# A graph network's two attention layers: the sums over edge slots move from VectorE reductions to identity products of TensorE in PSUM

## The chip, the cores and the metric

The kernel runs on one core of a Trainium2 chip. The metric is the device time of one execution in microseconds (us). The kernel before has a median of 5291.32 us over 3 runs, which lie between 5290.82 and 5300.97 us. The engines that matter here are TensorE (PE in the profile; its weight loads have a row of their own, PEld), VectorE (DVE), ScalarE (ACT) and GpSimd (POOL), which issues the gathers.

## The reference

Four message-passing layers run one after the other over the same graph of 3125 nodes and 100000 edges, each followed by a residual sum and a layernorm. Layers 0 and 1 are not touched. Layer 2 is attention with four heads and an edge bias, layer 3 attention with one head and keys that depend on the edge's type. Cut to what matters:

```python
# layer 2 (H = 4 heads of 32)
attn = jnp.sum(Q[dst] * K[src], axis=-1) * SCALE + edge_attr @ We      # then leaky
attn_exp = jnp.exp(attn - jnp.max(attn))
attn_norm = attn_exp / jnp.maximum(jax.ops.segment_sum(attn_exp, dst, n)[dst], 1e-12)
agg = jax.ops.segment_sum(V[src] * attn_norm[:, :, None], dst, n)
# layer 3 (one head; k_t is the key after the matrix of the edge's type)
scores = jnp.sum(Q[dst] * k_t, axis=-1) / scale * mu[edge_type]
out = jax.ops.segment_sum(V[src] * softmax_over_dst(scores)[:, None], dst, N)
```

For every destination node the kernel has to sum the value rows of its incoming edges, each weighted by its softmax weight. That weighted sum is what the change rearranges.

## The kernel before

The nodes are sorted by degree and cut into 25 tiles of 128, one node to a partition. A node's edges become slots: tile t has `CAP[t]` slots (57 in the first tile, 21 in the last, 821 in all), and slot s of a tile holds the s-th edge of each of its 128 nodes. Slots are worked through in chunks of at most W = 8. Nodes with more edges than slots would be finished in a loop (`behind`), which makes no trip on these inputs: the profile has 821 gathers a layer.

For each slot GpSimd issues one indirect gather (L102) that brings a row of 256 floats, key and value, for each of the 128 nodes into the tile `kv`. Layer 2 has 8 `kv` buffers, layer 3 has 12, each of one chunk; a buffer comes free when its value half has been read. On VectorE a chunk then takes these steps: `qk`, keys times query (L1206 in layer 2, L1364 in layer 3); `lg`, the sum over the head's columns (L1207, L1365); then, once per run, the softmax bookkeeping (`weights`, L700 to L714, with the exponentials on ScalarE); and, per chunk again, `weigh` (L722 to L730), in which `msg` is value times weight (L725), `u` is the sum of `msg` over its slots (L729), and `u` is added to the tile's sum `accb` (L730). Before a run's messages `faded` (L720) multiplies `accb` by the correction for a grown maximum. The query `qp` and the weights `ex` lie in PSUM, `kv`, `msg`, `u` and `accb` in SBUF. `msg` has two buffers, `u` one.

A run is a softmax group: in layer 2 `segments` makes runs of at most three chunks, in layer 3 a run is a whole tile. In layer 2 each tile ends with `closing` (L1252 to L1266: transposes, two dense layers, layernorm) and `table3` (L1274 to L1290: the queries of layer 3 and the key and value rows for all eight edge types, by products of TensorE), and a scatter of these rows into `ktv_tab`, which GpSimd issues. In layer 3 each tile ends with a division, a layernorm, and a scatter into `out`, also by GpSimd; in the source it stands after the gathers of the next tile.

Nobody writes the order of instructions on an engine by hand: a scheduler interleaves them by its own costs, and each engine then runs its list strictly in order. So a gather that waits for a free `kv` buffer, or a scatter that waits for its rows, holds back every gather behind it, and a VectorE instruction that waits holds back all of VectorE's.

[...]

Of the kernel before, what the change touches and what calls it, by code (L numbers as in the profile page):

```python
# [8 lines left out]
F32 = mybir.dt.float32  # L9
# [9 lines left out]
P = 128  # L19
# [8 lines left out]
W = 8  # L28
# [59 lines left out]
def tile_gnn(ctx, tc, a, out):  # L88
# [629 lines left out]
    def faded(acc, corr, heads):  # L718
        acch = acc.rearrange("p (h d) -> p h d", h=heads)
        V.tensor_mul(acch, acch, corr.unsqueeze(2).to_broadcast([P, heads, D // heads]))  # L720

    def weigh(pool, acc, val, ex, n, heads):  # L722

        msg = pool.tile([P, W, D], F32, name="msg")
        V.tensor_tensor(msg[:, :n, :].rearrange("p s (h d) -> p s h d", h=heads),  # L725
                        val.rearrange("p s (h d) -> p s h d", h=heads),
                        ex.unsqueeze(3).to_broadcast([P, n, heads, D // heads]), op=OP.mult)
        u = pool.tile([P, D], F32, name="u", bufs=1)
        V.tensor_reduce(u, msg[:, :n, :].rearrange("p s d -> p d s"), AX.X, OP.add)  # L729
        V.tensor_add(acc, acc, u)  # L730

    def query(ps, q):

# [454 lines left out]
    with tc.tile_pool(name="l2", bufs=2) as wp, tc.tile_pool(name="l2s", bufs=1) as sp, \  # L1188
# [31 lines left out]
        def behind2(t, pl, mk, rl):  # L1220
            lg = wp.tile([P, max(CAP), H2], F32, name="lg")
            kv = rows2(query(ps1, qb[:, t, :]), pl, W, lg[:, :W])
            biased(pl, W, lg[:, :W], mk)
            ex = ps1.tile([P, max(CAP), H2], F32, name="ex")
            corr = softmax(wp, lg[:, :W], W, H2, m[:, t, :], l[:, t, :], ex[:, :W])
            faded(accb[:, t, :], corr, H2)
            weigh(wp, accb[:, t, :], kv[:, :, D:], ex[:, :W], W, H2)

        behind(wp, behind2)

# [38 lines left out]
        def table3(t):  # L1269


            of = wp.tile([P, NTY, P], F32, name="of", bufs=1)
            for k in range(NTY):
                V.tensor_scalar(of[:, k, :], ident, is_t[:, k, t:t + 1], None, op0=OP.mult)  # L1274
            xk_ps = ps1.tile([P, NTY, P], F32, name="xk_ps", tag="dense")
            T.matmul(xk_ps, xb[:, t, :], of, start=True, stop=True)  # L1276
            xkT = wp.tile([P, NTY, P], F32, name="xkT", bufs=1)
            A.activation(xkT, xk_ps, AF.Copy)
            p_ps = ps1.tile([P, 3 * D], F32, name="p_ps")
            for k in range(NTY):  # L1280
# [12 lines left out]

        for t in range(NT):
            qp = query(ps1, qb[:, t, :])
            for s0, s1, run in segments(t):
                lg = wp.tile([P, max(CAP), H2], F32, name="lg")
                parts = []
                for c0, w in run:
                    o = OFF[t] + c0  # L1300
                    parts.append(rows2(qp, pay_sb[:, o:o + w], w, lg[:, c0 - s0:c0 - s0 + w]))
                n, o = s1 - s0, OFF[t] + s0
                biased(pay_sb[:, o:o + n], n, lg[:, :n], mask[:, o:o + n])
                ex = ps1.tile([P, max(CAP), H2], F32, name="ex")
                corr, rest = weights(wp, lg[:, :n], n, H2, m[:, t, :], l[:, t, :], ex[:, :n])
                faded(accb[:, t, :], corr, H2)
                for (c0, w), kv in zip(run, parts):
                    weigh(wp, accb[:, t, :], kv[:, :w, D:], ex[:, c0 - s0:c0 - s0 + w], w, H2)
                rest()

            rl = wp.tile([P, H2], F32, name="rl")
            V.tensor_scalar(rl, l[:, t, :], 1e-12, None, op0=OP.max)
            V.reciprocal(rl, rl)
            closing(t, rl)
            table3(t)
# [34 lines left out]
    with tc.tile_pool(name="l3", bufs=2) as wp, tc.tile_pool(name="l3s", bufs=1) as sp, \  # L1350
# [17 lines left out]
        def behind3(t, pl, mk, rl):  # L1368
            lg = wp.tile([P, max(CAP), 1], F32, name="lg")
            kv = rows3(query(ps1, qb[:, t, :]), pl, W, lg[:, :W, 0])  # L1370
            V.tensor_add(lg[:, :W, 0], lg[:, :W, 0], mk)
            ex = ps1.tile([P, max(CAP), 1], F32, name="ex", bufs=2)
            corr = softmax(wp, lg[:, :W], W, 1, m[:, t, :], l[:, t, :], ex[:, :W])
            faded(accb[:, t, :], corr, 1)
            weigh(wp, accb[:, t, :], kv[:, :, D:], ex[:, :W], W, 1)

        behind(wp, behind3)

# [1 line left out]
        for t in range(NT):  # L1380
            n = CAP[t]
            qp = query(ps1, qb[:, t, :])
            lg = wp.tile([P, max(CAP), 1], F32, name="lg")
            parts = []
            for s0, w in chunks(t):
                o = OFF[t] + s0
                parts.append(rows3(qp, pay_sb[:, o:o + w], w, lg[:, s0:s0 + w, 0]))
            V.tensor_add(lg[:, :n, 0], lg[:, :n, 0], mask[:, OFF[t]:OFF[t + 1]])
            ex = ps1.tile([P, max(CAP), 1], F32, name="ex", bufs=2)
            if to_put is not None:  # L1390

                unordered("out", scatter(out, od.ids(to_put[0]), to_put[1], bounds_check=N - 1, oob_is_err=False),
                          "nodes differ")
            corr, rest = weights(wp, lg[:, :n], n, 1, m[:, t, :], l[:, t, :], ex[:, :n])
            faded(accb[:, t, :], corr, 1)
            for (s0, w), kv in zip(chunks(t), parts):
                weigh(wp, accb[:, t, :], kv[:, :w, D:], ex[:, s0:s0 + w], w, 1)
            rest()
            rl = wp.tile([P, 1], F32, name="rcl")
            V.tensor_scalar(rl, l[:, t, :], 1e-10, None, op0=OP.add)  # L1400
            V.reciprocal(rl, rl)  # L1401
            y = wp.tile([P, D], F32, name="y")
            V.scalar_tensor_tensor(y, accb[:, t, :], rl, xb[:, t, :], op0=OP.mult, op1=OP.add)  # L1403
            o = wp.tile([P, D], F32, name="o")
            layernorm(wp, o, y, t)
            to_put = t, o
# [20 lines left out]
```

## Time and profile before

| what | value |
|---|---|
| median of 3 runs | 5291.32 us |
| profiled execution | 5349.01 us |
| its span, first to last instruction | 5347.3 us |
| DVE busy over the span | 3023.3 us (57%) |
| POOL busy over the span | 2812.4 us (53%) |
| PE busy over the span | 2126.7 us (40%) |
| gathers of layer 2, first to last | from 2806.4 to 4013.9 us |
| gathers of layer 3, first to last | from 4112.5 to 5286.7 us |
| sums `u` (L729) in both layers | 228 reductions, 384.1 us |

The profiled execution is 58 us (1.1%) slower than the median, so a sum made on the profile is carried over to the median by a factor of 0.99. Layers 0 and 1 end shortly before 2806 us. From there on there are four stretches: layer 2's gathers, the end of layer 2 after its last gather, layer 3's gathers, and the end after the last gather. In the profile a row of a group gives the busy time, the mean time of one instruction in ns, and after the bar the idle time of the engine just before these instructions, with what ended most of it. "remote" and "issue" are releasers that the profile cannot name. In a timeline the columns are start, duration, engine, line, operation, tiles, count, and in brackets the idle time before.

### The profile page before, as it was taken

The page shows a single profiled execution, that of the slowest core. Times are in us where ns is not written, and L with a number is a line of the kernel's source. Part 1 is how long each engine was busy: PE and PEld are TensorE (multiplying, and loading weights), DVE is VectorE, ACT ScalarE, POOL GpSimd, SP SyncE. Part 2 cuts the span into 40 slices and gives each one's busy share as a digit, 9 for nine tenths or more (in the row PEclk, how much of TensorE's full clock was granted, in tenths as well). Part 3 has the DMA queues.
Part 4 walks back from the last instruction along what each step waited for, and adds up shares of the span by engine and source line. Part 5 has one row for each costly group of instructions (what it writes and reads, how often), then busy time and mean ns, then how long its engine had stood idle before and what let it go on. Part 6 is the DMA issues. An engine that isn't in the chain of part 4 may idle for free. (4 is left out here: it accounts for less than half of the span.)

```text
span 5347.3 us, 40354 instructions
## 1 busy us (share of the span) xinstructions
PE 2126.7 (40%) x11946; PEld 1387.3 (26%) x12091; DVE 3023.3 (57%) x7369; ACT 985.1 (18%) x2562; POOL 2812.4 (53%) x2897
## 2 busy tenths in 40 slices
PE   7256767765666676776660121222323000000000
PEld 5134545544444444454330010011111000000000
DVE  8346665664555566555424566666664454454656
ACT  1023332322232333232110011111111000000000
POOL 0545545555353443444017666666662777666664
PEclk9577887777777778777885555555556555555555
DMA  2423323333222222333333333333331333223332
GB/s 84 121 72 86 95 75 91 89 92 87 79 83 77 79 82 69 89 85 86 148 137 104 102 98 114 103 105 106 121 113 61 105 98 92 86 85 92 89 88 60
DMA packets 213055, 498.40 MB, mean 93 GB/s; under 512 B 62329, under 2 KB 109100, under 8 KB 208185
## 3 DMA queue, kind: packets, MB, share of 16 engines
q0 software_dynamic: 136448, 397.65, 25.9%
q1 hardware_dynamic: 76344, 97.76, 5.7%
q8 instruction: 102, 1.67, 0.1%
q14 instruction: 161, 1.32, 0.1%
HBM read 424.65 MB, written 70.63 MB: 93 GB/s over the span
## 5 line engine op out<-in xcount | busy, mean ns | idle before, releaser
L102 POOL DMA_INDIRECT hs<-h_tab,srcx x821 | 844.9, 1029 | 839.2 <-issue 392.4
L102 POOL DMA_INDIRECT kv<-kv_tab,pay_sb x821 | 782.2, 953 | 372.2 <-issue 245.2
L102 POOL DMA_INDIRECT kv<-ktv_tab,pay_sb x821 | 803.0, 978 | 320.0 <-issue 243.7
L729 DVE TENSOR_REDUCE u<-msg 128x128 f32<-128x1024 f32 (+4 forms) x228 | 384.1, 1685 | 161.2 <-remote 100.0
L880 PE MATMUL zps<-oh,zq 128*128 128x512 bf16 x1099 | 357.7, 438 | 41.4 <-DVE bn_sd L751 10.1
L831 PE MATMUL lg<-yw,low 128*128 128x8 f32 x1642 | 234.7, 269 | 175.9 <-issue 88.6
L102 POOL DMA_INDIRECT zs<-z_tab,rel x205 | 208.8, 1019 | 172.9 <-DVE az L851 56.7
L831 PEld LDWEIGHTS lg<-yw,low 128*128 128x128 f32 x1642 | 228.6, 212 | 224.5 <-issue 107.1
L893 DVE TENSOR_TENSOR hs<-hs,t_ps 128x408 f32<-128x408 f32 (+1 forms) x231 | 122.1, 529 | 283.3 <-remote 165.8
L892 PE MATMUL t_ps<-zw,zT 128*128 128x136 f32 x1232 | 224.3, 311 | 127.5 <-DVE hs L893 78.9
L622 ACT ACTIVATE c_oha<-c_oha,srclo 128x50 bf16<-128x50 bf16 (+2 forms) x821 | 205.8, 346 | 250.1 <-DVE c_oha L570 147.0
L725 DVE TENSOR_TENSOR msg<-kv,ex 128x1024 f32<-128x1024 f32 (+4 forms) x228 | 248.8, 1103 | 3.1 <-issue 2.5
L884 PE MATMUL pre<-zT,zw 128*128 128x512 f32 x308 | 203.6, 748 | 89.0 <-ACT zT L882 44.3
L892 PEld LDWEIGHTS t_ps<-zw,zT 128*128 128x128 f32 x1232 | 193.4, 212 | 159.3 <-DVE hs L893 109.2
L740 PE MATMUL tp<-ident,an 128*128 128x128 f32 x25 | 11.5, 459 | 525.2 <-DVE qk L1206 257.0
L648 PE MATMUL c_ps<-c_ohs,c_ohd 128*128 128x128 bf16 x1300 | 128.6, 247 | 211.2 <-ACT c_sb L650 92.2
L886 PEld LDWEIGHTS pre<-ident,hs 128*128 128x128 f32 x1232 | 189.1, 221 | 74.0 <-issue 71.6
L1276 PE MATMUL xk_ps<-of,xqb 128*128 128x512 f32 x50 | 51.9, 1141 | 386.3 <-DVE xqb L758 239.6
L829 ACT ACTIVATE low<-pre 128x512 f32<-128x512 f32 (+2 forms) x215 | 123.2, 574 | 421.8 <-PE pre L886 148.0
L822 PE MATMUL pre<-identb,hq 128*128 128x512 bf16 (+3 forms) x645 | 199.3, 408 | 2.1 <-ACT hq L814 0.8
L886 PE MATMUL pre<-ident,hs 128*128 128x128 f32 x1232 | 194.5, 305 | 0.4 <-issue 0.4
L1364 DVE TENSOR_TENSOR qk<-kv,qp 128x1024 f32<-128x1024 f32 (+4 forms) x114 | 126.5, 1110 | 114.9 <-DMA kv<-ktv_tab,pay_sb 98.4
(397 smaller groups left out, 5206.3 us busy)
## 6 DMA issues: line engine op xcount, KB each, us to landing
rb<-rel_tab SPq DMA_DIRECT2D x77, 256.0 KB
c_tab<-c_sb SPq DMA_DIRECT2D x25, 768.0 KB
cs<-c_tab SPq DMA_DIRECT2D x6, 3200.0 KB
hs<-h_tab,srcx POOLq DMA_INDIRECT x821
kv<-kv_tab,pay_sb POOLq DMA_INDIRECT x821
kv<-ktv_tab,pay_sb POOLq DMA_INDIRECT x821
h_tab<-h SPq DMA_DIRECT2D x25, 132.0 KB
zs<-z_tab,rel POOLq DMA_INDIRECT x205
```

Of the source, the lines that this page charges most:

```text
L102: return G.indirect_dma_start(out=dst, out_offset=None, in_=table, in_offset=indirect(idx), **kw)
L622: A.activation(oha[:, s // 2, 0, :, s % 2], oha[:, s // 2, 1, :, s % 2], AF.Copy, scale=srclo[:, o:o + 1])
L648: T.matmul(cps[:, j * P:(j + 1) * P], ohd[:, b // 2, :, b % 2], ohs[:, b // 2, :, b % 2], start=(i == 0), stop=(i == nb - 1))
L725: V.tensor_tensor(msg[:, :n, :].rearrange("p s (h d) -> p s h d", h=heads), val.rearrange("p s (h d) -> p s h d", h=heads), ex.unsqueeze(3 ...
L729: V.tensor_reduce(u, msg[:, :n, :].rearrange("p s d -> p d s"), AX.X, OP.add)
L822: T.matmul(pre[:, :k], hq[:, i, :], identb.unsqueeze(1).to_broadcast([P, k, P]), start=(i == 0), stop=False)
L831: T.matmul(lg_ps[:, s, :], low[:, s, :], yw8, start=True, stop=True)
L880: T.matmul(zps, zq[:, i, 2 * R * k2:2 * R * (k2 + 1)], ohs[i][:, cols], start=(i + k2 == 0), stop=(i == NK - 1 and k2 == 1))
L884: T.matmul(pre[:, :k], zw[:, :D], zT[:, cols], start=False, stop=False)
L886: T.matmul(pre[:, s, :], hs[:, s0 + s, :D], ident, start=False, stop=(s == k - 1))
L892: T.matmul(t_ps[:, s, :], zT[:, (s0 + s) * P:(s0 + s + 1) * P], zw[:, D:], start=True, stop=True)
L1364: V.tensor_mul(qk[:, :n], kv[:, :n, :D], qp.unsqueeze(1).to_broadcast([P, n, D]))
```

## The change

`weigh` no longer reduces and adds on VectorE. It makes `msg` as before, and then one TensorE product per slot, with the 128x128 identity as the weights and `msg` of that slot as the moving operand (both float32), adds the slot into a PSUM bank `u_ps`. The first product of a run starts the bank, the last one stops it. VectorE adds `u_ps` to `accb` once per run. In layer 3 the fading of `accb` and the addition become one instruction. To have a bank for `u_ps` in layer 2, `p_ps` moves into the two banks of `e_ps`. `u_ps` has one buffer in layer 2 and two in layer 3.

```diff
-    def weigh(pool, acc, val, ex, n, heads):
+    def weigh(pool, u_ps, val, ex, n, heads, first, last):
 
         msg = pool.tile([P, W, D], F32, name="msg")
         V.tensor_tensor(msg[:, :n, :].rearrange("p s (h d) -> p s h d", h=heads),
                         val.rearrange("p s (h d) -> p s h d", h=heads),
                         ex.unsqueeze(3).to_broadcast([P, n, heads, D // heads]), op=OP.mult)
-        u = pool.tile([P, D], F32, name="u", bufs=1)
-        V.tensor_reduce(u, msg[:, :n, :].rearrange("p s d -> p d s"), AX.X, OP.add)
-        V.tensor_add(acc, acc, u)
+        for s in range(n):
+            T.matmul(u_ps, ident, msg[:, s, :], start=(first and s == 0), stop=(last and s == n - 1))
...
-            p_ps = ps1.tile([P, 3 * D], F32, name="p_ps")
+            p_ps = ps1.tile([P, 3 * D], F32, name="p_ps", tag="e_ps", bufs=2)
...
                 faded(accb[:, t, :], corr, H2)
+                u_ps = ps1.tile([P, D], F32, name="u_ps")
                 for (c0, w), kv in zip(run, parts):
-                    weigh(wp, accb[:, t, :], kv[:, :w, D:], ex[:, c0 - s0:c0 - s0 + w], w, H2)
+                    weigh(wp, u_ps, kv[:, :w, D:], ex[:, c0 - s0:c0 - s0 + w], w, H2, c0 == s0, c0 + w == s1)
                 rest()
+                V.tensor_add(accb[:, t, :], accb[:, t, :], u_ps)
...
             corr, rest = weights(wp, lg[:, :n], n, 1, m[:, t, :], l[:, t, :], ex[:, :n])
-            faded(accb[:, t, :], corr, 1)
+            u_ps = ps1.tile([P, D], F32, name="u_ps", bufs=2)
             for (s0, w), kv in zip(chunks(t), parts):
-                weigh(wp, accb[:, t, :], kv[:, :w, D:], ex[:, s0:s0 + w], w, 1)
+                weigh(wp, u_ps, kv[:, :w, D:], ex[:, s0:s0 + w], w, 1, s0 == 0, s0 + w == n)
             rest()
+            V.scalar_tensor_tensor(accb[:, t, :], accb[:, t, :], corr, u_ps, op0=OP.mult, op1=OP.add)
```

The loops `behind2` and `behind3` are changed in the same way.

More of the change, by code (lines that the diff above doesn't have):

```diff
@@ L1226, in behind2 @@
             faded(accb[:, t, :], corr, H2)
-            weigh(wp, accb[:, t, :], kv[:, :, D:], ex[:, :W], W, H2)
+            u_ps = ps1.tile([P, D], F32, name="u_ps")
+            weigh(wp, u_ps, kv[:, :, D:], ex[:, :W], W, H2, True, True)
+            V.tensor_add(accb[:, t, :], accb[:, t, :], u_ps)
         behind(wp, behind2)
@@ L1306, in tile_gnn @@
                 faded(accb[:, t, :], corr, H2)
+                u_ps = ps1.tile([P, D], F32, name="u_ps")
                 for (c0, w), kv in zip(run, parts):
-                    weigh(wp, accb[:, t, :], kv[:, :w, D:], ex[:, c0 - s0:c0 - s0 + w], w, H2)
+                    weigh(wp, u_ps, kv[:, :w, D:], ex[:, c0 - s0:c0 - s0 + w], w, H2, c0 == s0, c0 + w == s1)
                 rest()
+                V.tensor_add(accb[:, t, :], accb[:, t, :], u_ps)
             rl = wp.tile([P, H2], F32, name="rl")
@@ L1374, in behind3 @@
             faded(accb[:, t, :], corr, 1)
-            weigh(wp, accb[:, t, :], kv[:, :, D:], ex[:, :W], W, 1)
+            u_ps = ps1.tile([P, D], F32, name="u_ps", bufs=2)
+            weigh(wp, u_ps, kv[:, :, D:], ex[:, :W], W, 1, True, True)
+            V.tensor_add(accb[:, t, :], accb[:, t, :], u_ps)
         behind(wp, behind3)
@@ L1394, in tile_gnn @@
             corr, rest = weights(wp, lg[:, :n], n, 1, m[:, t, :], l[:, t, :], ex[:, :n])
[L1395 removed]
+            u_ps = ps1.tile([P, D], F32, name="u_ps", bufs=2)
             for (s0, w), kv in zip(chunks(t), parts):
[L1397 removed]
+                weigh(wp, u_ps, kv[:, :w, D:], ex[:, s0:s0 + w], w, 1, s0 == 0, s0 + w == n)
             rest()
+            V.scalar_tensor_tensor(accb[:, t, :], accb[:, t, :], corr, u_ps, op0=OP.mult, op1=OP.add)
             rl = wp.tile([P, 1], F32, name="rcl")
```

## The prediction

> **What bounds the kernel now.** I read the page's slices first. Layers 2 and 3 are the right half: TensorE is nearly or wholly idle there, its clock is at half, and POOL and VectorE share the work.
>
> ```profile
> PE   7256767765666676776660121222323000000000
> DVE  8346665664555566555424566666664454454656
> POOL 0545545555353443444017666666662777666664
> PEclk9577887777777778777885555555556555555555
> ```
>
> Next the stretches of the two layers: layer 2's gathers, its end, layer 3's gathers, the end.
>
> ```profile
> 2806.00:4015.00 1209.00, 268.04 (x493) 119.31 (x493) 723.01 (x1544) 149.19 (x331) 803.04 (x842) 0.56 0.36 107
> 4015.00:4112.00 97.00, 43.82 (x85) 19.08 (x85) 57.08 (x141) 21.63 (x43) 3.89 (x4) 0.66 0.12 46
> 4112.00:5288.00 1176.00, 0.00 (x0) 0.00 (x0) 600.55 (x928) 47.25 (x112) 824.62 (x842) 0.50 0.32 93
> 5288.00:5347.00 59.00, 0.00 (x0) 0.00 (x0) 46.51 (x93) 5.23 (x11) 3.98 (x4) 0.50 0.02 6
> ```
>
> The columns are length, then busy time (count) of PE, PEld, DVE, ACT, POOL, then PEclk, DMA share, GB/s. Neither engine looks full, so I ask for POOL's and VectorE's groups in each stretch (layer 2 first in both fences).
>
> ```profile
> L102 POOL DMA_INDIRECT kv<-kv_tab,pay_sb x821 | 782.2, 953 | 372.2 <-issue 245.2 <-DVE bn_mv L749 33.1 <-DVE msg L725 28.6
> L102 POOL DMA_INDIRECT kv<-ktv_tab,pay_sb x821 | 803.0, 978 | 320.0 <-issue 243.7 <-remote 32.1 <-DVE msg L725 19.8
> ```
> ```profile
> L729 DVE TENSOR_REDUCE u<-msg 128x128 f32<-128x1024 f32 (+4 forms) x106 | 179.3, 1692 | 62.3 <-remote 40.8 <-issue 13.2 <-DVE bn_st L747 1.5
> L730 DVE TENSOR_TENSOR accb<-accb,u 128x128 f32<-128x128 f32 x106 | 30.1, 284 | 20.4 <-remote 6.7 <-DVE sm L712 3.0 <-DVE lg L1216 2.4
> L729 DVE TENSOR_REDUCE u<-msg 128x128 f32<-128x1024 f32 (+4 forms) x104 | 175.6, 1688 | 98.5 <-remote 59.2 <-issue 18.8 <-DVE msg L725 14.4
> L1364 DVE TENSOR_TENSOR qk<-kv,qp 128x1024 f32<-128x1024 f32 (+4 forms) x109 | 120.9, 1109 | 114.9 <-DMA kv<-ktv_tab,pay_sb 98.4 <-issue 14.9
> L730 DVE TENSOR_TENSOR accb<-accb,u 128x128 f32<-128x128 f32 x104 | 30.0, 288 | 51.5 <-remote 26.7 <-DVE sm L712 5.8 <-issue 5.4
> ```
>
> A gather costs POOL 0.949 us (median) plus 0.30 us of issue, 1.254 us in all; 821 make 1030 us. With 21 scatters (0.99 + 0.30 us in layer 2, 1.03 + 0.30 in layer 3) POOL's floor is 1057 us in layer 2, and 1058 us in layer 3 plus 24 us by which its gathers are stretched (978 against 949 ns). The stretches last 1209 and 1176 us: POOL loses 152 and 94 us, in about 35 waits of 2 to 15 us, for a `kv` buffer or for rows to scatter. VectorE gives both.
>
> VectorE is the partner because it stands still far more than its busy share says. The timeline, with gathers running and after the last:
>
> ```profile
> 4587.49 1.09 POOL L102 DMA_INDIRECT kv<-ktv_tab,pay_sb  x1 [0.30 <-issue]
> 4587.89 1.87 DVE L729 TENSOR_REDUCE u<-msg 128x128 f32<-128x1024 f32 x1 [2.61 <-remote]
> ...
> 5301.34 0.28 DVE L725 TENSOR_TENSOR msg<-kv,ex 128x128 f32<-128x128 f32 x1
> 5301.54 1.86 DVE L729 TENSOR_REDUCE u<-msg 128x128 f32<-128x1024 f32 x1
> 5303.32 0.17 DVE L712 TENSOR_REDUCE sm<-ex 128x1 f32<-128x25 f32 x1
> 5303.44 0.29 DVE L730 TENSOR_TENSOR accb<-accb,u 128x128 f32<-128x128 f32 x1
> ```
>
> While gathers are issued, an instruction that needs the result of an earlier VectorE instruction starts up to 3 us late; once they have ended the same instructions follow without a gap. Of 1176 us in layer 3 VectorE idles 575, only 98 of them for data. So each dependent VectorE step costs its time and about 0.5 to 1 us more (98.5/104 before `u`, 51.5/104 before the sum).
>
> [...] `u` has one SBUF input and 98.5 us of idle time before it. [...] what holds VectorE back I leave open. [...] PEclk is 0.50 in layer 3, and two float32 products take
>
> ```profile
> 3350.39 0.64 PE L1263 MATMUL h_ps<-wm,oT 128*128 128x128 f32 x2
> 2122.74 1.11 PE L886 MATMUL pre<-ident,hs 128*128 128x128 f32 x8
> ```
>
> Each product is two records. Cold, the second starts 0.64 - 0.42 = 0.21 us after the first: 0.43 us a product[...]. Warm, (1.11 - 0.28)/7 = 0.12 us a record: 0.24 us a product. Weight loads run under them.
>
> **What goes.** Layer 2: `u` 179.3 + 62.3, sum 30.1 + 20.4, together 292 us of VectorE's 1209. Layer 3: 175.6 + 98.5, 30.0 + 51.5, and `faded` 6.8 + 2.5: 365 us of 1176. After the last gathers: 12.7 + 2.3 and 16.4 + 2.9 us, without idle time.
>
> **What comes on VectorE.** 46 sums in layer 2 by 0.29 us, 13 us; 23 fused ones in layer 3 by 0.35 us (the like of L1403, 349 ns), 8 us. [...] Without waits for TensorE, and without the waits for data (55 and 98 us, which are slack), VectorE needs 1209 - 55 - 292 + 13 = 875 us in layer 2, 1176 - 98 - 365 + 8 = 721 in layer 3. Both are below POOL's floor.
>
> **What comes on TensorE.** 821 products a layer: 350 us cold, 195 warm. Layer 3 has room, since TensorE does nothing there; layer 2 has 268 us of its own, so at most 620 of 1209. Throughput is no limit. The waits are: with two `msg` buffers the third message of a run waits for the products of the first, and the sum waits for all. Behind it VectorE's whole list stands, with `qk` of later chunks, and so POOL. A full chunk's products take 3.4 us cold, as long as VectorE's old chunk (1.21 + 1.87 + 0.28). In layer 3 the scheduler has put `qk` of the next tile between the messages; these wait for data that come every 10 us, and 33 products need 14, so I take 1 us a tile (0 to 5). In layer 2 the sum of one run stands some 7 us of VectorE work after its last message against 24 x 0.43 = 10 us of products; that of the other run has `xk_ps`, `p_ps` (8 records of 0.64 us) and ScalarE copies between its products, some 12 us against 7. That is 7 us a tile, 154 us for 22 tiles; bounds 0 (warm array) and 250. VectorE then has 875 + 154 = 1029 us against POOL's 1057: close enough that part of POOL's waits stays. I let 60 of 152 us stay: -92.
>
> **What moves.** In layer 3 the scheduler now places each scatter to `out` 7 to 17 gathers behind the last gather whose data stand ahead of its rows in VectorE's list; before it was 25 to 58. That is 9 to 21 us for a landing (2.4), a `qk` (1.2) and 2 to 12 dependent steps of 1 to 1.5 us, 6 to 20 us in all. So the scatter, and the gathers behind it, wait 0 to 5 us a tile, 0 to 100 us; I take 30, and keep the 24 us of stretch: -64. `p_ps` in the banks of `e_ps` waits for nothing: the bank's last reader is a tile old, some 40 us. Six more table loads of ScalarE (1.28 us each) hide under POOL.
>
> **The two ends.** After layer 2's last gather VectorE has about 50 us of backlog, without a gap; 15 us of it go, 8 more since it lags less, 6 come back for the last products: -17. The last stretch: 19 us go, 5 for less lag, and 21 cold products of the last tile (9 us) come: -15. The last tile's chain through `closing` and `table3` (30 us) is untouched.
>
> Sum: 92 + 64 + 17 + 15 = 188 us, of a profiled 5349; by 5291/5349, 186 us of the median: **5105 us**.
>
> **Rivals.**
> 1. TensorE takes the place of what goes. VectorE stands at the sums in layer 2 for the upper bound, and 5 us a tile in layer 3: 875 + 250 is over POOL's floor, 1125 plus data waits of 55 is 1180; layer 3 keeps 60 of 94. Gain 29 + 34 + 25 = 88: about 5205. For it: the array at half clock. Against: the `kv` buffers hold 64 or 96 gathers, so that waits of a few us even out.
> 2. POOL runs free: no waits left but 20 us a layer, ends shortened by 25 each. 132 + 74 + 50 = 256: about 5038. For it: VectorE's slack in both sums.
> 3. Slower: the `out` scatter. It holds back all gathers behind it. Layer 2 and the ends bring 124 us; once the waits of layer 3 reach 94 + 124 = 218 us, 10.4 us for each of 21 scatters, all of it is gone; at 14 us each the time is some 5365. For it: the margin fell from 25 to 58 gathers to 7 to 17. Against: a waiting POOL lets VectorE run without gaps, which ends the wait.
> 4. The sums were hidden anyway and the time stays (5280 to 5302). Against: POOL's waits end at VectorE's instructions.
>
> **Chances and range.** Forecast (5060 to 5160) 0.48; first rival (5160 to 5280) 0.20; second (4970 to 5060) 0.20; fourth 0.04; third 0.08. The bounds of the unknown waits give 5000 to 5240 for 8 in 10. Two runs differ from no change when they are over 0.2%, 11 us, apart: faster 0.88, same 0.04, slower 0.08.
>
> **What would show it.** POOL's idle time in layer 2 falls from 372 to about 300 us, in layer 3 from 320 to about 270, with gathers still at 0.95 us; VectorE's busy time falls to some 530 and 400 us in the two stretches; PE shows 821 products a layer at about 0.43 us in layer 3. I am wrong if the `out` scatter gathers more than 60 us of waits, if VectorE waits for `u_ps` more than 8 us a tile in layer 2, or if the self-waits move to other steps instead of going.

## The result, and the profile after

The changed kernel takes 5503.72 us (median of 4 runs, 5493.11 to 5518.24), beside 5296.15 us for the kernel before (5290.82 to 5311.01): a ratio of 1.0389, 95% interval 1.0356 to 1.0422. The forecast was 5105 us; the kernel is slower by 208 us. The profiled execution took 5518.24 us, with a span of 5516.2.

Times in this case depend on the chip, and no number below can be read without that. The experiments ran in five groups, each on one chip with the kernel before beside it. In the first two groups (chips 10 and 5) the kernel before takes 5300.66 and 5305.23 us, as in the result above; in the last three (chips 1, 9 and 2) it takes 4390.80, 4384.16 and 4385.60 us. I call them chips A and chips B. A ratio is always against the kernel before on the same chip.

The four stretches of the changed kernel, by the same view as before (length, then busy time and count of PE, PEld, DVE, ACT, POOL, then PEclk, DMA share, GB/s):

```profile
2783.50:4083.00 1299.50, 467.65 (x2025) 344.42 (x2025) 528.00 (x1378) 148.55 (x330) 799.77 (x842) 0.65 0.34 100
4083.00:4169.00 86.00, 49.52 (x195) 29.97 (x195) 44.26 (x128) 21.82 (x43) 3.96 (x6) 0.78 0.14 53
4169.00:5485.40 1316.40, 272.71 (x1532) 261.14 (x1532) 401.12 (x735) 52.59 (x118) 799.34 (x843) 0.58 0.29 83
5485.40:5516.20 30.80, 15.71 (x113) 15.33 (x111) 17.72 (x58) 6.31 (x11) 2.99 (x3) 0.78 0.04 9
```

Layer 2's gathers take 91 us more (1299.5 against 1208.5), layer 3's 141 more (1316.4 against 1175.2); the two ends are 12 and 29 us shorter. From the first gather of layer 2 on that is 192 us more, near the 208 of the medians. That layer 2 begins 23 us earlier says nothing of the change: with layers 0 and 1 unchanged it begins anywhere from 2749 to 2806 us in the profiles on chips A, and the latest of these is the one of the kernel before. VectorE did get rid of its work: 528 us for 723 in layer 2, 401 for 601 in layer 3. It has about three tenths less to do, and the stretches last longer.

The groups of layer 3 say where it stands (busy, mean ns, then idle time before and what ended it):

```profile
L102 POOL DMA_INDIRECT kv<-ktv_tab,pay_sb x821 | 777.0, 946 | 283.8 <-issue 248.9 <-DVE msg L725 19.4 <-ACT qp L734 15.2
L725 DVE TENSOR_TENSOR msg<-kv,ex 128x1024 f32<-128x1024 f32 (+4 forms) x107 | 117.7, 1114 | 442.5 <-remote 424.0 <-issue 10.5 <-PE u_ps L729 7.6
L105 POOL DMA_INDIRECT out<-o,node_d x22 | 22.4, 1017 | 248.5 <-DVE o L757 219.6 <-DVE l L714 20.7 <-DVE l L713 6.1
L1404 DVE SCALAR_TENSOR_TENSOR accb<-accb,corr,u_ps 128x128 f32<-128x128 f32 x22 | 7.6, 345 | 249.0 <-remote 243.1 <-PE u_ps L729 5.8
```

VectorE waits 442.5 us before `msg`, which needs a buffer that TensorE has read, and 249.0 us before the fused sum, which needs `u_ps`: 691 us in front of things that only TensorE can give. POOL then waits 248.5 us for `o`, 11 us for each scatter, before 43.6. In layer 2 the same shows at the other handoffs from TensorE, on ScalarE too:

```profile
L1275 DVE TENSOR_SCALAR of<-ident,is_t 128x128 f32<-128x128 f32 x84 | 23.7, 297 | 160.5 <-remote 156.9 <-PE xk_ps L1277 1.9 <-PE u_ps L729 1.7
L1312 DVE TENSOR_TENSOR accb<-accb,u_ps 128x128 f32<-128x128 f32 x45 | 12.8, 284 | 192.6 <-remote 177.4 <-PE u_ps L729 11.6 <-PE xk_ps L1277 3.5
L1284 ACT ACTIVATE qkv<-p_ps 128x384 f32<-128x384 f32 x21 | 10.3, 490 | 267.4 <-remote 240.5 <-PE p_ps L1282 21.3 <-PE u_ps L729 5.5
```

Two of these three handoffs were there before the change, and POOL issued the same gathers then. In layer 2 of the kernel before they were prompt:

```profile
L1274 DVE TENSOR_SCALAR of<-ident,is_t 128x128 f32<-128x128 f32 x84 | 23.6, 286 | 0.0
L1283 ACT ACTIVATE qkv<-p_ps 128x384 f32<-128x384 f32 x21 | 10.2, 487 | 58.5 <-issue 40.0 <-PE p_ps L1281 18.5
```

The 58.5 us are the time of the products themselves: wherever ScalarE waited there, it took the result 0.04 us after TensorE's last product ended (18 waits). So gathers alone do not make TensorE's handoffs late in this layer. They became late once TensorE carried the sums.

"Remote" means that the profile finds no instruction that ended near the end of the wait. The timeline of one tile of layer 3 shows why it finds none:

```profile
4730.10 0.94 PE L729 MATMUL u_ps<-msg,ident 128*128 128x128 f32 x6 [4.25 <-DVE msg L725]
4730.34 0.95 POOL L102 DMA_INDIRECT kv<-ktv_tab,pay_sb  x1 [0.30 <-issue]
...
4731.90 0.55 DVE L1367 TENSOR_TENSOR qk<-kv,qp 128x384 f32<-128x384 f32 x1 [0.55 <-DMA kv<-ktv_tab,pay_sb]
...
4760.35 0.95 POOL L102 DMA_INDIRECT kv<-ktv_tab,pay_sb  x1 [0.30 <-issue]
4761.60 0.95 POOL L102 DMA_INDIRECT kv<-ktv_tab,pay_sb  x1 [0.30 <-issue]
4768.61 0.35 DVE L1404 SCALAR_TENSOR_TENSOR accb<-accb,corr,u_ps 128x128 f32<-128x128 f32 x1 [36.16 <-remote]
```

The tile's last products end at 4731.04. The sum that waits for nothing else starts at 4768.61, 36 us after VectorE was free. Nearly all that time POOL issues gathers, one every 1.25 us; then POOL stands, because it has come to the scatter of `o`, and 6 us later the sum starts. The products are not slow (six records in 0.94 us); word of their end comes late. The trace has the updates of the semaphores too: the one that ends this wait is TensorE's and stands at 4768.58, and for 681 of the 691 us an update of TensorE's stands at the end of the wait in the same way. I measured, for each instruction of VectorE and ScalarE that waits for TensorE, how long after TensorE's last end, or after its own engine was free, it started: in layer 3 28 were over 1 us late, 638 us together. All eleven that were over 30 us late ended only after POOL had stood still for 3.6 to 8.7 us; of the shorter ones many ended while POOL was issuing. And the self-waits are gone: VectorE's idle time before instructions that wait for its own result alone fell from 431 to 1 us in layer 3 and from 377 to 7 in layer 2.

### The profile page after: what moved, and what is told of

Its sections match the earlier page's. It is cut to its first block, busy times and chain, and to the rows that moved or that the text cites. A ratio compares the mean times of both kernels' runs of the same rounds, so it can differ in the third digit from the quotient of the medians.

```text
span 5516.2 us, 46597 instructions
## 1 busy us (share of the span) xinstructions
PE 2625.8 (48%) x15375; PEld 1889.0 (34%) x15375; DVE 2587.3 (47%) x6962; ACT 990.7 (18%) x2568; POOL 2781.7 (50%) x2897
## 5 line engine op out<-in xcount | busy, mean ns | idle before, releaser
L729 PE MATMUL u_ps<-msg,ident 128*128 128x128 f32 x3284 | 550.3, 340 | 1339.6 <-DVE msg L725 971.4
L729 PEld LDWEIGHTS u_ps<-msg,ident 128*128 128x128 f32 x3284 | 532.4, 253 | 1400.0 <-DVE msg L725 991.9
L102 POOL DMA_INDIRECT kv<-ktv_tab,pay_sb x821 | 777.0, 946 | 283.8 <-issue 248.9
L879 PE MATMUL zps<-oh,zq 128*128 128x512 bf16 x1232 | 390.0, 437 | 32.6 <-DVE oh L870 19.6
L102 POOL DMA_INDIRECT zs<-z_tab,rel x205 | 207.9, 1014 | 173.7 <-DVE az L850 59.6
L870 DVE TENSOR_SCALAR oh<-rb,relid 128x1024 bf16<-128x1024 f16 x308 | 146.5, 491 | 95.6 <-remote 39.2
```

What stands on the lines that cost most here:

```text
L102: return G.indirect_dma_start(out=dst, out_offset=None, in_=table, in_offset=indirect(idx), **kw)
L729: T.matmul(u_ps, ident, msg[:, s, :], start=(first and s == 0), stop=(last and s == n - 1))
L870: V.tensor_scalar(oh[:, :n * P], rb[:, :n * P], relid[:, i:i + 1], None, op0=OP.is_equal)
L879: T.matmul(zps, zq[:, i, 2 * R * k2:2 * R * (k2 + 1)], ohs[i][:, cols], start=(i + k2 == 0), stop=(i == NK - 1 and k2 == 1))
```

## Theories

**H, late handoffs:** while POOL issues gathers back to back, the signal that a TensorE instruction is done reaches its waiters late. The loss is the sum of these waits. **R, rate:** the float32 products are too slow. **O, order:** the scatter to `out` stands too early in POOL's list (the third rival of the prediction), and the rest follows from that.

## The experiments

**Products behind the last one.** If TensorE keeps back a signal because it falls idle, a few more products should push it out.

```diff
+    def fill(junk, msg):
+        for k in range(4):
+            T.matmul(junk, ident, msg, start=True, stop=True)
...
+                fill(u2_ps[:, 1, :], msg[:, w - 1, :])
```

> Four more products of the last message slice, into PSUM columns that nobody reads, behind the last product of each run in both layers (49 x 4 in layer 2, 25 x 4 in layer 3); the output is unchanged. Theory H (a product's completion reaches its waiter late when TensorE falls idle behind it while POOL issues gathers; this is the loss): if a following product lets the completion out, VectorE's idle time before the fused sum of layer 3 falls from 249 us to under 60, and the time falls from 5504 to some 5200 to 5300 us. If the completion is late whatever follows, the time stays within 20 us of 5504. Theory R (the products are too slow): 5504 plus 49 x 1.7 us of more products in layer 2 and 25 x 1.7 us in layer 3, as far as they hold up the next run: 5510 to 5600 us. Theory O (the earlier place of the scatter to out): layer 3 unchanged, 5504.

Measured on a chip A: 5520.28 us, 1.0423 (1.0378 to 1.0469). VectorE's idle time in layer 3 is 503.7 us before `msg` and 216.2 before the sum, 720 us together against 691. Four more products behind the last one do not push the signal out.

**No sums at all.** The products and the additions are left out in both layers; only the fading stays.

```diff
-        for s in range(n):
-            T.matmul(u_ps, ident, msg[:, s, :], start=(first and s == 0), stop=(last and s == n - 1))
...
-            V.scalar_tensor_tensor(accb[:, t, :], accb[:, t, :], corr, u_ps, op0=OP.mult, op1=OP.add)
+            V.tensor_scalar(accb[:, t, :], accb[:, t, :], corr, None, op0=OP.mult)
```

> The sums over the slots are left out altogether in layers 2 and 3 (neither products nor additions; the messages are still computed, the output lacks the neighbours' part). Theory H: without a product to wait for, nothing is handed over late in layer 3; VectorE loses 292 and 365 us of work as I had costed it; POOL sets the pace with 1057 us a layer: 5020 to 5110 us. Theory O: the scatter to out stays in its earlier place with its waits of 11 us, so layer 3 keeps some 1290 us and the time is 5250 to 5400 us. Theory R: as H. If VectorE's own self-waits come back in layer 3 (they were gone in the changed kernel), about 1 us for each dependent step, the stretch of layer 3 stays above 1130 us.

Measured on the same chip: 5232.86 us, 0.9886 (0.9835 to 0.9938). This is the most surprising run: with the whole subject of the change gone (and the output with it), 68 us are gained, where I had forecast 186 from a part of it. The gathers of layer 3 and of layer 2, the scatters to `out`, and the reader of `p_ps` in layer 2:

```profile
L102 POOL DMA_INDIRECT kv<-ktv_tab,pay_sb x821 | 843.7, 1028 | 293.2 <-issue 292.2 <-DMA kv<-ktv_tab,pay_sb 1.0
L102 POOL DMA_INDIRECT kv<-kv_tab,pay_sb x821 | 778.8, 949 | 401.1 <-issue 247.0 <-DVE msg L725 88.1 <-remote 27.0
L105 POOL DMA_INDIRECT out<-o,node_d x22 | 23.9, 1088 | 7.0 <-issue 6.7 <-DVE accb L1397 0.3
L1280 ACT ACTIVATE qkv<-p_ps 128x384 f32<-128x384 f32 x22 | 10.5, 478 | 15.9 <-issue 14.2 <-PE p_ps L1278 1.7
```

In layer 3 POOL waits for no other engine, but its gathers grow from 978 to 1028 ns and take back most of what the waits had cost: 1153.6 us against 1175.2. In layer 2 next to nothing is gained (1200.5 us against 1208.5): VectorE loses 178 us of busy time, and its self-waits grow from 377 to 485 us although there are fewer steps. The scatters to `out` stand at the same gather in POOL's list as in the changed kernel or up to 14 gathers earlier, and wait 7 us in all: the place alone costs nothing, and O falls. And without the sums TensorE's handoffs in layer 2 are prompt again (15.9 us before `qkv` instead of 267.4), although `p_ps` lies in the banks of `e_ps` as in the changed kernel: that move is not what makes them late.

**Products that nobody needs.** The kernel before, with its sums on VectorE, and 821 products in layer 3 beside them.

```diff
-        msg = pool.tile([P, W, D], F32, name="msg")
+        msg = pool.tile([P, W, D], F32, name="msg", bufs=4 if heads == 1 else 2)
...
         V.tensor_add(acc, acc, u)
+        if junk is not None:
+            for s in range(n):
+                T.matmul(junk, ident, msg[:, s, :], start=True, stop=True)
```

> The kernel before, with 821 products of the messages in layer 3 beside its own sums on VectorE, into a PSUM bank that nobody reads, and with four msg buffers instead of two in layer 3. Theory H: nobody waits for the products (but a msg buffer four chunks later), so VectorE loses nothing to them, unless their completions hold the buffers: layer 3 within 40 us of its 1176 and the time 5290 to 5340 us. If the mere presence of products moves VectorE's self-waits away (451 us before, 25 us in the changed kernel), layer 3 falls to some 1090 us and the time to about 5210. Theory R or a contention of TensorE's reads with the gathers: layer 3 rises towards 1316 us, the time towards 5430.

Measured on the same chip: 5363.28 us, 1.0116 (1.0083 to 1.0149). The groups of layer 3:

```profile
L729 DVE TENSOR_REDUCE u<-msg 128x128 f32<-128x1024 f32 (+4 forms) x104 | 177.6, 1708 | 0.9 <-DVE msg L725 0.7 <-issue 0.2
L725 DVE TENSOR_TENSOR msg<-kv,ex 128x1024 f32<-128x1024 f32 (+4 forms) x104 | 114.4, 1110 | 574.3 <-remote 444.9 <-issue 125.9 <-PE junk L733 3.5
L733 PE MATMUL junk<-msg,ident 128*128 128x128 f32 x1482 | 254.4, 350 | 969.9 <-remote 555.1 <-issue 232.3 <-DVE msg L725 179.2
```

Not quite what H had said, which allowed 40 us more for layer 3 unless the buffers are held, nor the hope for VectorE's self-waits: VectorE waits 574 us for `msg` buffers that the products of four chunks earlier still hold, and its idle time before `u` falls from 98.5 to 0.9 us. Layer 3 takes 1226.5 us, 51 more. TensorE's own row adds a second loss: it waits 555 us for word of its own earlier products before it goes on, so that here the products too come late. A reader that frees a buffer is a handoff like any other, and four buffers do not cover it.

**The scatter later.** The rows of a tile scattered one tile later, with four `o` buffers.

```diff
-            if to_put is not None:
+            if len(to_put) > 1:
+                t1, o1 = to_put.pop(0)
...
-            to_put = t, o
+            to_put.append((t, o))
```

> The changed kernel, with the scatter of a tile's rows to out issued one tile later (about 33 gathers more between the rows and the scatter; four o buffers). Theory O: the 248 us of POOL's waits before these scatters go, and layer 3 falls from 1316 to about 1100 us: 5270 to 5310 us. Theory H: VectorE waits for TensorE all the same; the scatter no longer waits, POOL runs on until the kv buffers are full and waits there: idle time before the gathers of layer 3 rises from 284 by 100 us or more, and the time falls by no more than 100 us, to 5400 to 5500 us. If it is POOL's standing still that lets the completion out, the waits for the fused sum get longer than their present 11 us a tile.

Measured on the same chip: 5497.49 us, 1.0368 (1.0318 to 1.0417); the scatters still wait 237.2 us. By itself it decides little: the scheduler moved the first eleven scatters, by 5 to 19 gathers, and left nearly all others where they were. What speaks against O is the run without sums.

**Layer 3 without POOL's gathers.** SyncE issues 821 plain transfers of the same size in their place (other rows, so another output), in both kernels.

```diff
-                gather(kv[:, s, :], ktv, pl[:, s, 2:3])
+                r = (o + s) % 200 * P
+                nc.sync.dma_start(kv[:, s, :], ktv[r:r + P])
```

> The changed kernel with the 821 gathers of layer 3 replaced by plain transfers of the same size and number that SyncE issues (128 consecutive rows of the same table, so wrong rows: the output of layer 3 is another); POOL issues nothing there but the scatters to out. Theory H (completions are late because POOL issues gathers back to back): VectorE's idle time before the messages and the fused sum of layer 3, 691 us in the changed kernel, falls under 60 us, and what is left is the products' own time; the stretch of layer 3 is shorter than that of plain_before by 60 us or more. Theory R (the products are too slow, or the semaphores of TensorE are): VectorE still waits over 300 us for TensorE. Time: layer 3 lasts 450 to 900 us instead of 1316, as the transfers allow.

> The kernel before with the same replacement in layer 3. Theory H: VectorE's self-waits of layer 3 (431 us before instructions that need only VectorE's own result) vanish to under 30 us, since POOL no longer issues; layer 3 lasts as long as VectorE is busy (642 us) or as the transfers take, whichever is longer. If the self-waits are VectorE's own affair, they stay at 300 us or more.

Measured on the other chip A, one run each: 4630.44 us with the change and 4698.72 without. From the first `qk` of layer 3 to the last it takes 423.4 us with the change and 597.2 without. The groups of the changed kernel, then those of the kernel before:

```profile
L725 DVE TENSOR_TENSOR msg<-kv,ex 128x1024 f32<-128x1024 f32 (+4 forms) x108 | 117.8, 1105 | 11.1 <-PE u_ps L729 9.6 <-issue 1.0
L1405 DVE SCALAR_TENSOR_TENSOR accb<-accb,corr,u_ps 128x128 f32<-128x128 f32 x23 | 7.9, 342 | 1.9 <-PE u_ps L729 1.5
```
```profile
L729 DVE TENSOR_REDUCE u<-msg 128x128 f32<-128x1024 f32 (+4 forms) x108 | 181.0, 1676 | 0.0
L730 DVE TENSOR_TENSOR accb<-accb,u 128x128 f32<-128x128 f32 x108 | 30.7, 284 | 0.0
```

This decides between H and R. The same products, three times as dense in time, with more bytes moving (255 GB/s against 83), and VectorE waits 13 us for TensorE instead of 691. In layer 2 of the same execution, where POOL gathers as ever, it waits 302 us in front of `msg` and the sum (238 in the changed kernel). In the kernel before, the 150 us of idle time before `u` and its addition are gone as well: these were late signals of VectorE to itself. So lateness goes when POOL's gathers go, and the amount of traffic is not what causes it. The edit changes three things at once, though: the engine that issues, the queue, and the rows (consecutive ones instead of indirect ones); which of them counts is not shown. In this stretch, without gathers, the change takes off 174 us.

**Asking later.** Layer 3 alone, six `msg` buffers, and the fused sum taken only after the next tile's messages.

```diff
+        def close3(t, corr, u_ps, after):
+            V.scalar_tensor_tensor(corr, after, 0.0, corr, op0=OP.mult, op1=OP.add)
+            V.scalar_tensor_tensor(accb[:, t, :], accb[:, t, :], corr, u_ps, op0=OP.mult, op1=OP.add)
...
+                to_put = close3(*to_close, msg[:, 0, :1])
```

> Layer 2 as before; layer 3 with the sums on TensorE, but six msg buffers instead of two, and the fused sum and all behind it (to the rows of out) taken only after the messages of the next tile (a tiny VectorE instruction ties it there). The output is the reference's. Theory H with lateness of at most 38 us: a tile takes 47 us, so the completions have come when they are asked for; VectorE's idle time for TensorE in layer 3 falls from 706 to under 200 us, layer 3 from 1316 to 1150 to 1200 us, its end stays at 30 to 45 us; with layer 2 as before the time is 5260 to 5310 us. If lateness grows without bound while POOL issues (POOL's stand-stills are what ends it), the wait only moves: layer 3 stays above 1250 us and the time above 5350. Theory R: above 5350 too.

Measured: 5372.30 us, 1.0109 (1.0077 to 1.0140). The groups of layer 3:

```profile
L102 POOL DMA_INDIRECT kv<-ktv_tab,pay_sb x821 | 777.0, 946 | 266.4 <-issue 265.8 <-DVE lg L1377 0.3 <-DVE qk L1376 0.3
L725 DVE TENSOR_TENSOR msg<-kv,ex 128x1024 f32<-128x1024 f32 (+4 forms) x110 | 116.5, 1109 | 505.3 <-remote 399.6 <-issue 97.6 <-PE u_ps L729 8.0
L1395 DVE SCALAR_TENSOR_TENSOR accb<-accb,corr,u_ps 128x128 f32<-128x128 f32 x22 | 7.5, 342 | 82.3 <-remote 49.0 <-issue 33.3
L729 PE MATMUL u_ps<-msg,ident 128*128 128x128 f32 x1556 | 313.0, 339 | 969.0 <-issue 818.8 <-DVE msg L725 133.1 <-DVE qk L1376 7.0
```

The sum's own wait falls from 249 to 82 us, but the messages wait 505 us for their buffers, and layer 3 still takes 1268.9 us. The time lies in my second branch, but the row of TensorE shows something that neither branch had: TensorE itself is slow here. It stands idle 818.8 us before products without a wait that the profile shows, most of it (645 us) with the message already there. Between 4648 and 4690 us of this trace, for instance, one product record starts about every 2.8 us, where in the changed kernel six took 0.94. In part VectorE waits here for products that are really late. So the run does not tell whether a tile's distance would cover a late signal, and why TensorE goes at this pace is open.

**TensorE at the ends alone.** Sums on TensorE in the last tile of layer 2 and the last two of layer 3; `weigh_v` is the old `weigh`, with reduction and addition on VectorE.

```diff
+                if t == NT - 1:
+                    u_ps = ps1.tile([P, D], F32, name="u_ps")
...
+                else:
+                    for (c0, w), kv in zip(run, parts):
+                        weigh_v(wp, accb[:, t, :], kv[:, :w, D:], ex[:, c0 - s0:c0 - s0 + w], w, H2)
...
+            if t >= NT - 2:
+                u_ps = ps1.tile([P, D], F32, name="u_ps", bufs=2)
```

> The kernel before with the sums on TensorE only where POOL has hardly a gather left to issue: in the last tile of layer 2 and the last two of layer 3; all other sums on VectorE as before. Theory H: layers 2 and 3 keep 1208 and 1175 us, the stretch after the last gather of layer 2 falls from 98 to about 86 us and that of layer 3 from 60 to about 31: 5250 us, 0.992 of before. If a few late completions in tile 23 of layer 3 hold up POOL: up to 38 us of that is lost, 5250 to 5295.

Measured: 5298.35 us (22 runs), 0.9983 (0.9964 to 1.0001). The end of layer 2 took 91.9 us for 97.6, that of layer 3 59.9 for 59.6. So the 29 us that the changed kernel gained at its end did not come from the sums of the last tiles. My reading, which no run tests alone, is that its POOL had been held up more, so that VectorE had less left over when the last gather went.

**Chips without late handoffs.** The next groups fell on chips B. Their kernels were made for questions about lateness, and there is none there to ask about. The change in layer 3 alone, with `weigh_v` in all of layer 2:

> The change in layer 3 alone; layer 2 sums on VectorE as before. If the losses of the two layers are separate: layer 2 back at 1208 to 1225 us (1299 in the changed kernel), layer 3 at 1316 and its end at 31 us as in the changed kernel, so 5291 + 141 - 28 = 5404 us, up to 5425. If layer 3 lost only because layer 2 handed it over in another state, layer 3 is nearer to 1175 and the time near 5300.

The kernel before with one needless product per chunk of layer 3:

```diff
-                weigh(wp, accb[:, t, :], kv[:, :w, D:], ex[:, s0:s0 + w], w, 1)
+                u = weigh(wp, accb[:, t, :], kv[:, :w, D:], ex[:, s0:s0 + w], w, 1)
+                T.matmul(junk, ident, u, start=True, stop=True)
```

> The kernel before, with one product per chunk of layer 3 (104 in all, of u by the identity) into a PSUM bank that nobody reads; u has 24 buffers, so that VectorE meets such a product again only 24 chunks later. If a held completion of TensorE takes the place of VectorE's own (in the run with 821 products beside the old sums VectorE's self-waits fell from 431 to 18 us), the self-waits of layer 3 fall under 150 us, layer 3 to 1135 to 1160 us and the time to 5230 to 5280 us. If they vanished there only because VectorE stood waiting for TensorE, they stay at 350 to 431 us and the time at 5285 to 5330 us.

The changed kernel with pauses in POOL's issuing:

```diff
                 parts.append(rows3(qp, pay_sb[:, o:o + w], w, lg[:, s0:s0 + w, 0]))
+                G.memset(pause, 0.0)
```

> The changed kernel with a POOL memset of 128 x 2048 zeros (some 1.8 us by the 2.77 us of a 128 x 3200 one) after each chunk of up to 8 gathers of layer 3: POOL is as busy, but issues no DMA for 1.8 us out of 12. If back-to-back issuing of gathers is what holds TensorE's completions, they come out in these pauses or the few gathers after them: VectorE's idle time for TensorE in layer 3 falls from 706 to under 250 us, and layer 3 lasts POOL's 1058 + 24 + 103 x 1.9 = 1280 us, up to 1330. If any busy POOL holds them, or a pause has to be longer (5 to 9 us of standing still preceded most late completions), the waits stay over 500 us and layer 3 is 1316 + 100 to 200 us.

The kernel before with layer 3's chunk sums `us` added up once per tile:

```diff
-                weigh(wp, accb[:, t, :], kv[:, :w, D:], ex[:, s0:s0 + w], w, 1)
+                weigh(wp, None, kv[:, :w, D:], ex[:, s0:s0 + w], w, 1, us[:, i, :])
+            V.tensor_reduce(u, us[:, :len(parts)].rearrange("p s d -> p d s"), AX.X, OP.add)
+            V.scalar_tensor_tensor(accb[:, t, :], accb[:, t, :], corr, u, op0=OP.mult, op1=OP.add)
```

> The kernel before with layer 3's sums still on VectorE: each chunk's reduction goes to a slot of its own, and the slots are added up and faded once per tile (one reduction and one fused instruction instead of 104 additions and 25 fades): some 100 dependent VectorE steps fewer, 30 us of work and 50 us of idle time before it. Nothing waits for TensorE. With POOL's gathers at 1.0 to 1.03 us each when nothing holds it (as with the sums left out), layer 3 goes from 1175 to no less than 1153 us and its end from 60 to 55: 5265 to 5290 us, 0.995 to 1.0 of before.

Measured on chip 1: the change in layer 3 alone 4391.06 us, 1.0001 (0.9992 to 1.0009); one product per chunk that nobody needs 4384.45, 0.9987 (0.9980 to 0.9995); sums on VectorE added up once per tile 4389.29, 0.9993 (0.9984 to 1.0001); pauses in POOL 4564.42 (one run). Repeats on chips 9 and 2 gave 0.9998 for the first, 0.9992 and 0.9990 for the second, and for the pauses 4551.83 us (one run) and 1.0400. None of the four was seen on a chip A, so whether a pause lets the signals out, whether a late signal of TensorE replaces VectorE's own, and whether the losses of the two layers add up, stays open. The groups of layer 3 in the run with one needless product per chunk, whose VectorE work is that of the kernel before, on chip 9:

```profile
L102 POOL DMA_INDIRECT kv<-ktv_tab,pay_sb x821 | 778.7, 948 | 263.9 <-issue 259.9 <-DVE accb L730 0.9 <-DMA out<-o,node_d 0.6
L729 DVE TENSOR_REDUCE u<-msg 128x128 f32<-128x1024 f32 (+4 forms) x111 | 184.9, 1679 | 0.0
L730 DVE TENSOR_TENSOR accb<-accb,u 128x128 f32<-128x128 f32 x110 | 31.5, 286 | 0.0
```

The gathers are the ones of chips A, 948 ns and 0.3 us of issue. But POOL waits for nobody, and VectorE's dependent steps follow one another without a gap while gathers run.

**The change itself on such a chip.**

> The changed kernel itself once more. On a chip with late handoffs (kernel before about 5300 us): 1.039 of before, 5504 us. On a chip without (kernel before about 4391 us): both kernels stand at POOL's floor in layers 2 and 3 (1058 and 1056 us, 8 to 16 us of POOL's waits), so that VectorE's and TensorE's work there is hidden; what is left of the change is at the two ends, where the last tile's sums and products stand against each other: within 0.4% of before, 4375 to 4395 us.

Measured on chip 9: 4369.12 us, 0.9967 (0.9955 to 0.9980). It is faster there, by 15 us (0.3%). Its stretches and two groups of layer 3:

```profile
2152.40:3208.20 1055.80, 488.20 (x2066) 369.34 (x2066) 538.23 (x1427) 153.76 (x344) 799.62 (x842) 0.68 0.41 123
3208.20:3276.00 67.80, 39.44 (x154) 24.75 (x154) 27.17 (x80) 15.21 (x29) 3.94 (x5) 0.75 0.17 67
3276.00:4331.80 1055.80, 295.65 (x1552) 284.23 (x1552) 404.48 (x749) 54.58 (x122) 799.33 (x843) 0.61 0.36 104
4331.80:4360.10 28.30, 12.98 (x90) 12.79 (x90) 13.99 (x44) 4.33 (x8) 2.99 (x3) 0.68 0.04 10
```
```profile
L725 DVE TENSOR_TENSOR msg<-kv,ex 128x1024 f32<-128x1024 f32 (+4 forms) x108 | 117.0, 1103 | 5.0 <-PE u_ps L729 4.9
L105 POOL DMA_INDIRECT out<-o,node_d x22 | 22.4, 1018 | 6.7 <-issue 6.4 <-DVE lg L1368 0.3
L1404 DVE SCALAR_TENSOR_TENSOR accb<-accb,corr,u_ps 128x128 f32<-128x128 f32 x23 | 7.9, 342 | 4.3 <-PE u_ps L729 4.1
```

The same program, with the same products and with each scatter at the same gather, waits 9 us for TensorE in layer 3 and 7 us before the scatters. Both layers stand at 1055.8 us, POOL's own time. With VectorE's old sums they take 1058 us on chips B (layer 2 in the run with the change in layer 3 alone, 1058.2) and 1056 (layer 3 in the run with the needless products): the sums were hidden. Of the 15 us the profiles place 8 at the end of layer 2, 68 us against 76, and 2 in layer 2; the rest has no place that they show. The end of layer 3 gains nothing there: 28.3 us with the change, 28.2 in the run with one needless product per chunk.

No complete version with gathers that I ran beats both kernels on chips A by more than its interval; on chips B the changed kernel is the fastest of those run.

## Why the prediction was wrong

**POOL's floor** of 1057 us in layer 2 and 1058 in layer 3 was right to 4 us, on chips B, where nothing holds POOL. On chips A it could not be reached: in the run without sums layer 3 stays at 1153.6, since the stretch of the gathers, which I took as a fixed 24 us, became 821 x (1028 - 949) ns = 65 us, and POOL's issue time rose from 244 to 292 us (14 of them before the first gather).

**What goes** was right in busy time: VectorE's fell by 195 and 199 us, to 528 and 401 us, against "some 530 and 400". Wrong was to take the idle time before the removed steps along. I had written that each dependent step costs its time and 0.5 to 1 us more, and had left open what holds VectorE back. The idle time did not belong to the steps: without sums the self-waits of layer 2 grew from 377 to 485 us over fewer steps, and layer 2 lost only 8 us, where I had forecast 92 from cheaper sums. Nor do the 98.5 us of idle time before `u` belong to a reduction beside gathers: on chips B they are 0.0 with the same gathers (948 ns each), and on the chip A an update of VectorE's own semaphore, the signal of the step before, stands at the end of 77 of them.

**The step that failed** is "What comes on TensorE": the waits, 1 us a tile in layer 3 and 7 in layer 2. I priced them by how long the products take, with a handoff at no cost. The products took less than I said: 273 us busy in the stretch of layer 3, where the granted clock was 0.58 on average, against 350 at the 0.43 us of a product that I called cold, which was measured at a clock of 0.50 (the 0.24 us called warm at 1.00). The 28 late handoffs of layer 3 took 3 to 38 us, 23 on average. 23 us for layer 3 became 691. In layer 2 238 us stood before `msg` and the sum, 11 a tile, within the bound of 250 that I had set for another reason, but the handoffs that were there before, which I had left at nothing, added 160 us at one line alone. Where handoffs are prompt the price was right or too high: 9 us in layer 3, and in layer 2 12 us before `msg` and the sum instead of 154.

**What moves:** I took 30 us for the scatters to `out` and named more than 60 as a sign of error; it was 248.5. The third rival had the place and the sign (11 us a scatter, against its break-even of 10.4), though not the size (some 5365 us at 14 us a scatter, against 5504 measured), and not the cause: its mechanism was the scatter's place in POOL's list, and with the same place the waits are 7 us in the run without sums and 6.7 us on chip 9. The rows come late because the fused sum does. Its argument against itself, that a waiting POOL ends the wait, fits the eleven longest waits, only some 6 us after POOL has stopped.

**The two ends** gained 12 and 29 us, where 17 and 15 were forecast. That the second gained at all is luck: its reason, the sums of the last tile, is worth nothing in the run with TensorE at the ends alone, nor on chip 9.

**The rivals:** the first (TensorE takes the place of what goes) named what happened, with waits of 5 us a tile in layer 3 where 691 us make 28. The second (POOL runs free) and the fourth (hidden anyway) are what happens on chips B, together: POOL was free there already.

A sign was there in the profile of the kernel before. In the stretch of layers 0 and 1, where TensorE has much to do and feeds ScalarE while POOL gathers, ScalarE's waits (us in total, times, longest) were

```profile
ACT c_sb L650 <- remote: 136.4, 18, 19.1
...
ACT low L829 <- remote: 74.3, 13, 12.2
```

Single waits of 19 and 12 us for results of TensorE, with no instruction near that could have ended the wait. The forecast rests on layers 2 and 3 alone. There the trace gave no warning: in layer 3 TensorE had nothing to hand over, and in layer 2 what it handed over was prompt.

## What to carry to other kernels

Before work moves to another engine, price the handoff from that engine; the duration of its instructions is no substitute. A prompt handoff in the same stage is no proof either, since the work that moves can make it late, as in layer 2 here (58.5 us before `qkv` in the kernel before, 267.4 in the changed one). Look through the whole trace for waits on that engine that no instruction near explains, and let the range of the forecast cover them. Idle time before a dependent step need not be that step's own (without sums the self-waits of layer 2 went from 377 to 485 us): leave the work out altogether and see what is gained before estimating what a cheaper way would bring. Where an unexplained wait is what a change would save, measure on more than one chip.

## What was new about the hardware

On two of five chips, while POOL issued indirect transfers every 1.25 us, signals came late, and whose they were depended on the kernel and the stage. In layers 2 and 3 of the kernel before they were VectorE's: its results reached itself 0.86 us late on average (500 such steps in layer 3), while TensorE's in layer 2 were taken 0.04 us after their products. With the sums on TensorE they were TensorE's, which reached VectorE and ScalarE up to 44 us late, and VectorE's to itself were prompt (1 us in all of layer 3, 18 with the 821 products that nobody needs). In the run without sums layer 3 had neither (0.0 us before `msg`), and POOL's own gathers were 8% longer than 949 ns (1028). So the lateness moved rather than added up; what decides where it falls is not shown. On the other three chips, with gathers of the same length (947 to 952 ns), both engines' signals were prompt: 0.0 us before VectorE's sums in layer 2 of the change in layer 3 alone on chip 1, 9 us of waits for TensorE in layer 3 of the changed kernel on chip 9, 21 with the pauses on chip 2. On a chip A plain transfers at three times the rate caused next to none of it (13 us before `msg` and the sum, 0.0 before `u`; one run of each kernel). The kernel before takes 913 us more on chips A (5300 against 4387), some 600 of them before layer 2 begins (at 2749 to 2806 us in the profiles with unchanged layers 0 and 1, against 2152 to 2166 on chips B).

What in a chip, or in its condition at that time, makes the difference is open: the groups on chips A all came first, and in the profiles I found nothing that differs but the waits. Open too is whether a late product is held up inside TensorE after its recorded end, or only the word of it.
